# Graph attention, two layers: 52 instead of 46 edge tiles of layer 1 gathered early, their completion seven groups apart instead of eight

## The chip, the cores and the metric

The kernel runs on one core of one Trainium2 chip. The metric is the device time of one execution in microseconds (us). Nine runs of the kernel before gave a median of 2495.17 us, from 2488.37 to 2499.84. Engines are named as the profile names them: PE (TensorE matmul), PEld (TensorE weight load), DVE (VectorE), ACT (ScalarE), POOL (GpSimd), SP (SyncE, which here only issues DMAs).

## The reference, cut to what matters

6250 nodes with 768 features, 100,000 edges sorted by destination. Two layers of graph attention (4 heads, then 1), then a small MLP and a residual. A layer is:

```python
h = (x @ W).reshape(n, heads, -1)
e = leaky_relu(alpha_s[src] + alpha_d[dst], 0.2)
e = exp(e - segment_max(e, dst)[dst])
alpha = e / segment_sum(e, dst)[dst]
out = segment_sum(h[src] * alpha[:, :, None], dst)
```

The costly part is `h[src]`: for each of 100,000 edges a row of the layer's node table has to be fetched (268 numbers in layer 1, 259 in layer 2), weighted and added into its destination.

## The kernel before, in words

Nodes are cut into NT = 49 tiles of 128, edges into 782 tiles of 128. Four edge tiles make a **group** (196 groups per layer), two edge tiles a **pair**, and four groups belong to about one node tile, as edges are sorted by destination.

**Feature stage** (0 to about 172 us in the profile). For each node tile PE multiplies the normalised features with W1 (L457), ACT leaves the row in SBUF (`kept`, one tile for each node tile), and SP stores it to the layer's table in HBM (L484).

**Layer 1** (about 176 to 1309 us). POOL gathers the rows of each edge tile with one indirect DMA (L663), eight groups (AHEAD) before they are used, into a ring of 20 pair buffers `G`. DVE computes each pair's weights (L741, L751) and the weighted rows `hw` (L753, a ring of 8 pairs), and one-hot matrices of the destinations (`hot`, L691). PE adds each edge tile into its destinations with a one-hot matmul into `o_ps` (L765); an fp32 matmul is two MATMUL and two LDWEIGHTS records in the trace. Once in four groups PE also sums the destinations' factors with 16 small matmuls (`meet`, L709), and the node steps turn a finished node tile into its row for layer 2 (L963, L1016 and further). A buffer of G is free when DVE has made `hw` from it; a buffer of `hw` is free when PE has read it.

**Early gathers, the part that is changed.** While the features are still being computed, POOL has nothing else to gather. Some pairs of layer 1, listed in SOON, are therefore gathered then (`soon_rows`, L351, L357) from the part of the table that is already there: the entry SOON[i] = NT - m says that the last m node tiles are missing. Indices into the missing tiles are replaced by 0 (`soon_places`, L345). What is gathered is held in G buffers (16 pairs, SOON_HELD) or moved to HBM by SP (`soon_away`, L361, L364), all of it by the start of layer 1, and brought back by SP when its pair is due (`soon_back`, L366), so POOL skips that pair in `gather` (L651). What is missing is then added from `kept`, once for each of the pair's two edge tiles:

- `soon_hits` (L377, L383, DVE): m one-hot matrices of 128x128 that say which edge wants which node of a missing tile
- `soon_missing` (L388, L394, PE): m fp32 matmuls of 128x128 by 128x268 over the missing node tiles
- `soon_out` (L397, L400, ACT) copies the sum out of PSUM, and `soon_whole` (L402, L406, DVE) adds it to the gathered row.

The order on every engine is written out by hand in the loop over groups. SOON_GROUP[i] is the group whose second pair is the early pair i and at which its rows are made whole. Around it (`at`), the loop has:

```python
for k, hits_at in ((2 * i, at - 10), (2 * i + 1, at - 6)):
    if g == hits_at + 3 + (k % 2 == 0): soon_out(sm, k)
    if g == at: soon_whole(G, k)
    if g == hits_at: soon_hits(pre_pool, k)
    if g == hits_at + 1 + (k % 2 == 0): soon_missing(k)
if g == at - 13: soon_sources(pre_pool, i)
```

PSUM for `missing1`, for the node steps' `tp` and for their `h_ps` is one set of two buffers (tag "n").

**Layer 2** (about 1309 to 2475 us) gathers its 782 tiles in the same way (eleven of them early, in another manner, L334), puts the weight into the one-hot (L748), and ends each node tile with the MLP (L1129, L1139) and the output.

Of the kernel before, what the change touches and what calls it, by code (L numbers as in the profile page):

```python
# [27 lines left out]
NT = -(-N // P)  # L28
# [20 lines left out]
THERE = {layer: [there for n, there in stages for _ in range(n)] for layer, stages in EARLY.items()}  # L49


SOON = [NT - m for m in (11, 20, 2, 19, 11, 18, 3, 18, 4, 17, 4, 16, 5, 15, 10, 15, 7, 14, 13, 12, 9, 8,
                         6)]
SOON_GROUP = [8 * i + 11 for i in range(len(SOON))]
SOON_AT = {2 * g + 1: i for i, g in enumerate(SOON_GROUP)}
SOON_FROM, SOON_HELD = min(SOON), 16
BARE = 8
# [14 lines left out]
def kernel(  # L72
# [142 lines left out]
    def edge_places(ones):  # L215
# [5 lines left out]
        yield  # L221
        soonest = sorted(range(len(SOON)), key=SOON.__getitem__)
        for i in range(0, len(SOON), 2):
            for k in soonest[i:i + 2]:
# [112 lines left out]

    soon_i = const.tile([P, len(SOON), 2], I32, name="soon_i")
    soon_ok = const.tile([P, len(SOON), 2], F32, name="soon_ok")
    soon_d = dram.tile([len(SOON), P, 2 * TW[1]], F32, name="soon_d")  # L340
# [293 lines left out]
    def layer_edges(layer, H, node, pre, matched, pre_pool):  # L634
# [4 lines left out]
        with tc.tile_pool(name=f"eg{layer}", bufs=6) as eg, \  # L639
# [237 lines left out]
            for g in range(NG):  # L877
# [41 lines left out]
                if layer == 1:  # L919
                    for i, at in enumerate(SOON_GROUP):  # L920
                        for k, hits_at in ((2 * i, at - 10), (2 * i + 1, at - 6)):
# [565 lines left out]
```

## Time and profile before

| what | us |
|---|---|
| median of 9 runs | 2495.17 |
| the profiled execution's own time | 2497.29 |
| its span, first to last instruction | 2495.5 |
| around the span | 1.8 |
| PE busy, whole span | 1752.0 (70%) |
| POOL busy, whole span | 1526.4 (61%) |
| DVE busy, whole span | 1391.2 (56%) |
| ACT busy, whole span | 445.3 (18%) |

A row of the costliest groups gives line, engine and operation, tiles, shape and count, then the time the group was busy, the mean of one in ns, and after a second bar the engine's idle time just before these instructions with what ended it. "issue" there means that nothing which the profile shows was waited for, and "remote" that the releaser is not known. The mean granted TensorE clock of the whole run is 0.798 of full speed. Busy time of POOL is the gather instruction alone (0.95 us); between two gathers that wait for nothing lie another 0.30 us.

### The profile page before, as it was taken

The page shows a single profiled execution, that of the slowest core. Times are in us where ns is not written, and L with a number is a line of the kernel's source. Part 1 is how long each engine was busy: PE and PEld are TensorE (multiplying, and loading weights), DVE is VectorE, ACT ScalarE, POOL GpSimd, SP SyncE. Part 2 cuts the span into 40 slices and gives each one's busy share as a digit, 9 for nine tenths or more (in the row PEclk, how much of TensorE's full clock was granted, in tenths as well). Part 3 has the DMA queues.
Part 4 walks back from the last instruction along what each step waited for, and adds up shares of the span by engine and source line. Part 5 has one row for each costly group of instructions (what it writes and reads, how often), then busy time and mean ns, then how long its engine had stood idle before and what let it go on. Part 6 is the DMA issues. An engine that isn't in the chain of part 4 may idle for free.

```text
span 2495.5 us, 27029 instructions
## 1 busy us (share of the span) xinstructions
PE 1752.0 (70%) x7728; PEld 1280.3 (51%) x7729; DVE 1391.2 (56%) x4195; ACT 445.3 (18%) x1368; POOL 1526.4 (61%) x1666
## 2 busy tenths in 40 slices
PE   9961777777677775766674666676777677677677
PEld 7741555565465564655552444454454444444455
DVE  7742667666776676776772534443443444444444
ACT  6740011111111111111120011111111111111112
POOL 5257566666666666666625666666666666666661
PEclk9975888788788787887886767877876777777788
DMA  9986454555555554555524445544554545554552
GB/s 343 352 273 221 133 156 138 156 155 145 151 162 163 158 157 135 160 162 154 152 72 147 130 135 153 159 142 144 159 153 133 159 136 150 154 150 140 148 152 74
DMA packets 167330, 400.38 MB, mean 160 GB/s; under 512 B 36631, under 2 KB 54254, under 8 KB 167174
## 3 DMA queue, kind: packets, MB, share of 16 engines
q0 software_dynamic: 75072, 211.10, 31.9%
q1 hardware_dynamic: 90732, 185.99, 21.6%
q10 hardware_dynamic: 1370, 1.48, 0.2%
q8 instruction: 65, 1.06, 0.2%
q14 instruction: 91, 0.75, 0.1%
HBM read 333.87 MB, written 64.56 MB: 160 GB/s over the span
## 4 chain that ended last, share of the span: by engine, by line
PE 52%; issue 21%; DVE 11%; another core or an unknown queue 11%; ACT 3%; DMA 1%; POOL 1%; DVEq 0%; ACTq 0%; SPq 0%; POOLq 0%
PE o_ps L765 27%; PE missing L394 9%; PE y_ps L1139 6%; PE h_ps L457 4%; DVE hw L753 2%; PE tp L1129 2%; DVE hot L691 2%; DVE hw L748 1%; PE h_ps L1016 1%; PE e_parts L709 1%; PE y_ps L1078 1%; DVE factors L741 1%; DVE factors L751 1%; DVE acc L782 1%
## 5 line engine op out<-in xcount | busy, mean ns | idle before, releaser
L663 POOL DMA_INDIRECT G<-table,src_i x1507 | 1434.7, 952 | 788.6 <-issue 379.6
L765 PE MATMUL o_ps<-G,hw 128*128 128x258 f32 x1564 | 526.4, 463 | 223.7 <-issue 191.0
L765 PEld LDWEIGHTS o_ps<-G,hw 128*128 128x128 f32 x1564 | 350.4, 231 | 366.6 <-issue 275.6
L765 PE MATMUL o_ps<-hw,hot 128*128 128x260 f32 x1564 | 441.4, 423 | 104.6 <-issue 91.0
L753 DVE TENSOR_TENSOR hw<-G,factors 128x520 f32<-128x520 f32 x391 | 272.2, 696 | 287.5 <-remote 194.9
L765 PEld LDWEIGHTS o_ps<-hw,hot 128*128 128x128 f32 x1564 | 319.4, 209 | 187.9 <-issue 114.8
L394 PE MATMUL missing<-kept,soon_hit 128*128 128x268 f32 x1028 | 273.6, 416 | 64.0 <-issue 46.0
L748 DVE TENSOR_SCALAR hw<-iota_ps,dcol,w 128x128 f32<-128x128 f32 x782 | 284.9, 406 | 15.6 <-DVE w L744 1.3
L394 PEld LDWEIGHTS missing<-kept,soon_hit 128*128 128x128 f32 x1028 | 207.3, 204 | 118.0 <-issue 73.8
L791 ACT ACTIVATE sum<-acc 32x260 f32<-32x260 f32 (+1 forms) x384 | 160.0, 417 | 408.3 <-DVE acc L782 212.4
L1143 DVE TENSOR_TENSOR y<-y_ps,xt 128x384 f32<-128x384 f32 (+1 forms) x98 | 54.5, 556 | 265.5 <-PE o_ps L765 89.6
L1139 PE MATMUL y_ps<-wm,mT 128*128 128x384 f32 x392 | 184.1, 600 | 20.0 <-ACT mT L1134 12.2
L709 PE MATMUL e_parts<-win,mask 128*128 128x12 bf16 (+1 forms) x1564 | 68.2, 167 | 173.4 <-issue 169.3
L709 PEld LDWEIGHTS <-mask 128*128 128x128 bf16 x1564 | 61.8, 98 | 186.0 <-issue 174.6
L457 PE MATMUL h_ps<-w,r 128*128 128x264 f32 (+1 forms) x588 | 142.9, 398 | 14.8 <-issue 8.3
L691 DVE TENSOR_TENSOR hot<-iota_ps,dcol 128x512 f32<-128x512 f32 x196 | 133.5, 681 | 0.0
L457 PEld LDWEIGHTS h_ps<-w,r 128*128 128x128 f32 x588 | 111.9, 197 | 38.6 <-issue 10.0
L1139 PEld LDWEIGHTS y_ps<-wm,mT 128*128 128x128 f32 x392 | 78.3, 222 | 99.0 <-issue 54.1
L741 DVE TENSOR_TENSOR factors<-G,factors 128x8 f32<-128x8 f32 (+1 forms) x782 | 125.4, 160 | 4.4
L1134 ACT ACTIVATE mT<-tp,bm1c 128x128 f32<-128x128 f32 x98 | 30.6, 363 | 521.6 <-PE o_ps L765 175.5
L969 ACT ACTIVATE rT<-tp,bT 128x128 f32<-128x128 f32 x196 | 61.1, 364 | 277.9 <-remote 214.1
L782 DVE SCALAR_TENSOR_TENSOR acc<-acc,keep,o_ps 128x260 f32<-128x260 f32 (+1 forms) x192 | 91.3, 476 | 12.3 <-PE o_ps L765 7.7
(418 smaller groups left out, 1290.4 us busy)
## 6 DMA issues: line engine op xcount, KB each, us to landing
xt<-in_x SPq DMA_DIRECT2D x96, 384.0 KB
drow<-dmod_d SPq DMA_DIRECT2D x49, 512.0 KB
mask_d<-mask SPq DMA_DIRECT2D x97, 256.0 KB
mask<-mask_d SPq DMA_DIRECT2D x97, 256.0 KB
G<-table,src_i POOLq DMA_INDIRECT x1507
xTt<-in_xT SPq DMA_DIRECT2D x49, 384.0 KB
out<-y SPq DMA_DIRECT2D x48, 384.0 KB
table<-kept SPq DMA_DIRECT2D x49, 134.0 KB
```

The costliest lines, as they stand in the source:

```text
L394: nc.tensor.matmul(soon_p[k], hit[:, T - there], kept[T], start=(T == there), stop=(T == NT - 1))
L457: nc.tensor.matmul(h_ps[:, :n], r[:, k], w1[:, k, :n], start=(k == 0), stop=(k == KI - 1))
L663: nc.gpsimd.indirect_dma_start(out=G[k // 2][:, k % 2], out_offset=None, in_=table[layer], in_offset=bass.IndirectOffsetOnAxis(ap=src_i[:, ...
L691: nc.vector.tensor_tensor(hot[g][:, T[0]:T[0] + n], iota_ps.unsqueeze(1).to_broadcast([P, n, P]), dcol[:, k:k + n].unsqueeze(2).to_broadca ...
L709: nc.tensor.matmul(parts[t][:, at + k], m[:, k * P:(k + 1) * P], pre.win[:, 2 * u + 2], start=True, stop=True)
L741: nc.vector.tensor_mul(v, e2, rho)
L748: nc.vector.tensor_scalar(hw[:, t], iota_ps, dcol[:, k:k + 1], w[:, t], ALU.is_equal, ALU.mult)
L753: nc.vector.tensor_mul(hw, Gp[:, :, :RW[1]].rearrange("p t (h c) -> p t h c", h=H), w.unsqueeze(3).to_broadcast([P, 2, H, C + 1]))
L765: nc.tensor.matmul(o_ps[u], l, r[:, :RW[layer]], start=(g % 2 == 0 and k == 0), stop=(g % 2 == 1 and k == tiles(g)[-1]))
L782: nc.vector.scalar_tensor_tensor(acc, run[0], keep[:, u % 2:u % 2 + 1], o_ps.pop(u), ALU.mult, ALU.add)
L791: nc.scalar.activation(done[t][r], acc[r], AF.Copy)
L1139: nc.tensor.matmul(y_ps, mT[:, j], wm2[:, j, s * half:(s + 1) * half], start=False, stop=(j == KH - 1))
```

## The change

Three entries are added to SOON and the list is arranged anew; the early pairs stand 7 instead of 8 groups apart. Nothing else in the code is changed.

```diff
-SOON = [NT - m for m in (11, 20, 2, 19, 11, 18, 3, 18, 4, 17, 4, 16, 5, 15, 10, 15, 7, 14, 13, 12, 9, 8,
-                         6)]
-SOON_GROUP = [8 * i + 11 for i in range(len(SOON))]
+SOON = [NT - m for m in (11, 20, 2, 20, 3, 19, 4, 18, 4, 18, 5, 17, 7, 17, 10, 16, 11, 15, 15, 14, 13, 13,
+                         12, 9, 8, 6)]
+SOON_GROUP = [7 * i + 11 for i in range(len(SOON))]
```

That makes 26 pairs (52 edge tiles) instead of 23 (46). The missing node tiles add up to 307 instead of 257, so `soon_missing` has 614 matmuls instead of 514. The most for one pair stays 20, so the buffers keep their sizes. The early pairs stand in groups 11 to 186 (11 to 187 before). On POOL the compiled program has 52 early gathers (46) and 730 gathers in layer 1 (736); the gathers of layer 2 are unchanged. On SP it has three more stores of early rows, three more loads of them and three more loads of source indices.

## The prediction

> **What bounds the kernel now.** I read the busy table by stretches first, then the gather row and the matmul rows of the costliest groups, then the waits of PE and of DVE, then PE and POOL side by side in order of time. The first view is busy time by stretches: three of layer 1 (early, middle, late), then three of layer 2; the number behind an engine's time counts its instructions.
>
> ```profile
> core 0: us, PE busy (x) PEld busy (x) DVE busy (x) ACT busy (x) POOL busy (x), PEclk, DMA share, GB/s
> 260.00:600.00 340.00, 254.74 (x1155) 197.06 (x1154) 232.81 (x593) 48.29 (x161) 215.15 (x226) 0.82 0.53 149
> 600.00:930.00 330.00, 243.75 (x1149) 191.10 (x1148) 226.46 (x592) 52.74 (x182) 209.74 (x221) 0.83 0.55 157
> 930.00:1272.00 342.00, 232.84 (x1134) 189.04 (x1133) 232.73 (x611) 51.65 (x178) 219.02 (x231) 0.82 0.53 150
> 1371.00:1700.00 329.00, 224.05 (x919) 147.84 (x919) 148.01 (x560) 43.63 (x114) 216.95 (x228) 0.76 0.49 144
> 1700.00:2050.00 350.00, 250.62 (x1028) 167.27 (x1028) 157.10 (x596) 51.32 (x135) 229.95 (x242) 0.76 0.50 148
> 2050.00:2440.00 390.00, 274.49 (x1165) 183.78 (x1164) 174.73 (x658) 59.84 (x159) 255.49 (x270) 0.78 0.51 151
> ```
>
> No engine is full in any stretch. Now the waits, PE's and then DVE's, from 260 to 1260 us (us in total, times, longest).
>
> ```profile
> PE e_parts L709 <- issue: 120.4, 84, 2.6
> PE o_ps L765 <- issue: 72.9, 58, 2.4
> PE missing L394 <- issue: 46.0, 47, 2.2
> ...
> PE o_ps L765 <- DVE hw L753: 1.7, 1, 1.7
> ```
> ```profile
> DVE hw L753 <- remote: 183.1, 41, 7.1
> DVE hw L753 <- PE o_ps L765: 37.6, 15, 5.8
> ```
>
> PE hardly waits for DVE's `hw`; DVE waits for PE to free `hw` buffers; POOL's extra waits are for G buffers, on DVE. So everything hangs on PE, and PE's idle time is "issue": nothing that it waits for. What that is shows in order of time, PE then POOL:
>
> ```profile
> 1021.91 1.92 PE L765 MATMUL o_ps<-hw,hot 128*128 128x260 f32 x8
> 1023.67 0.27 PE L709 MATMUL e_parts<-win,mask 128*128 128x12 bf16 x5
> 1025.62 0.17 PE L709 MATMUL e_parts<-win,mask 128*128 128x12 bf16 x1 [1.68 <-issue]
> ...
> 1036.15 0.17 PE L709 MATMUL e_parts<-win,mask 128*128 128x12 bf16 x1 [1.24 <-issue]
> 1038.24 0.27 PE L709 MATMUL e_parts<-win,mask 128*128 128x12 bf16 x4 [1.92 <-issue]
> ```
> ```profile
> 1034.18 0.94 POOL L663 DMA_INDIRECT G<-table,src_i  x1 [0.30 <-issue]
> 1039.41 0.94 POOL L663 DMA_INDIRECT G<-table,src_i  x1 [4.28 <-DVE hw L753]
> ```
>
> From 1023.9 PE crawls, 0.7 to 2.8 us from one small matmul to the next, and at 1038.2 it is back at full pace, 3.1 us after POOL fell idle at 1035.1 because its ring was full. The same order returns at almost every long crawl (stalls that end at 680.4, 948.4, 993.7, 1127.9; POOL idle from 676.9, 945.4, 990.5, 1124.8). After a POOL pause PE runs about 100 to 140 records, then crawls until the next pause. So POOL's time and the pauses that PE needs make the length. That gives a law to calculate with: a gather costs 1.25 us (0.95 busy and 0.30 between), and the rest of a stretch is pause. By the six rows: 340 - 226 x 1.25 = 57.5 us for 2309 PE and PEld records, 24.9 ns a record; then 53.8 for 2297 (23.4), 53.3 for 2267 (23.5), 44.0 for 1838 (23.9), 47.5 for 2056 (23.1), 52.5 for 2329 (22.5). Two layers with different PE work agree within a tenth: 308.6 us for 13,096 records, **23.6 ns of pause for each PE record**.
>
> **The change part by part.**
>
> *Removed: six gathers of layer 1* (736 to 730) on POOL's path: 6 x 1.25 = **-7.5 us**.
>
> *Added: 100 matmuls of missing tiles* (514 to 614), each two MATMUL and two LDWEIGHTS records, 400 in all: 400 x 23.6 ns = **+9.4 us**. No row shows this price by itself, so both ends: below, 0, as the seven cycles between long crawls from 934 to 1245 us last 42.2 to 46.7 us and do not follow the number of missing tiles in them. Above, all of it on PE: the row of L394 has 273.6 us for 1028 MATMUL records, 266 ns each, 200 x 266 = 53 us. I take the law, since its six rows are nearest.
>
> The Trainium skill, "Runtime: NRT & Kernel Launch", section "Instruction fetch mechanics", says that an engine's instructions are streamed in 16 KiB blocks of 256 by a queue of its own while earlier ones run, so that crossing a block is mostly hidden. The trace agrees on the blocks (queue q8 has 65 packets, 1.06 MB), but not that PE's issue is smooth. By that rule the 400 records would cost nothing and the sum below would be -4.1 us instead of +5.3.
>
> *Moved into the feature stage: six early gathers and three stores to HBM.* 6 x 134 KB and 3 x 268 KB are 1.6 MB. From 100 to 150 us the DMA share is 0.99 to 1.01 at 304 to 341 GB/s, so at most 1.6 MB / 341 GB/s = 4.7 us; at least 0, for POOL has some 20 us of waits beyond the 0.30 between its early gathers (100.5 to 172.3 us), and the share is 0.72 from 150 on. From 100 to 172 us PE is busy 57.5 of 72 us, and one tile's twelve matmuls at 135 us take 5.65 instead of 2.84 us: 17 us lost, while the 46 gathers and seven stores move 8.0 MB; the same share for 1.6 MB is 17 x 1.6 / 8.0 = **+3.4 us**, which I take. Each added row waits for its table store, as before; what queues behind the stores on SP are the later x loads and table stores, and they are inside this price.
>
> *Beside other work:* DVE's `soon_hits`, 75.2 us for 514 matrices, 146 ns each, 100 more are 14.6 us; six L406 at 486 ns, 2.9 us. DVE has 183 + 38 us of waits for PE in this stretch; without that cover they would cost the 17.5 us. ACT: six copies of 393 ns, ACT is busy 165.5 us of layer 1's 1115.7. SP's three loads back and three of indices, 1.2 MB at a DMA share of 0.53. A load back waits for a G buffer, and SP's mask stores and `drow` loads queue behind it, but POOL waits for the same ring, and `drow` comes four node tiles ahead.
>
> *The new distance.* With 8 groups the early pairs stand at one phase to the node steps (every 4 groups), with 7 it drifts. Both use PSUM tag "n", where PE's waits for ACT in layer 1 are 10.6 + 5.4 + 5.0 = 21 us. They could vanish or double, so +-21; I take 0, as PE time that is not in the pause law is taken back from the crawl.
>
> Sum: -7.5 + 9.4 + 3.4 = **+5.3 us**. The profiled execution took 2497.3, so 2502.6 in its frame; it stood 2.1 above the median, so **2501 us** against 2495.17. About 0.2% (5 us) is what a measurement can tell from no change.
>
> **The rivals.**
>
> *A, faster: the pauses belong to POOL's full ring, not to PE's records.* The ring fills whether or not PE has more to do, the added matmuls only shorten the crawl that would come anyway, and the six gathers are pure gain. For it: the cycles above do not shrink when the missing tiles fall from 27 to 14 a cycle; the crawls grow instead (14.0 to 16.8 us). Against it: the same 23.6 ns in layer 2, where no tile is missing. It decides where a record costs under (7.5 - 3.4) / 400 = 10 ns. Price: -7.5 and nothing in the feature stage, 2488; if each of the three pairs also spares a wait of its own of 2.5 us, 2480.
>
> *B, slower: the pauses belong to the early pairs.* From 1024 on each 8-group cycle has one pause of about 4.3 us at the crawl and one of about 3 us after the skipped pair, some 7 us together beyond the 0.30s. With 26 cycles instead of 23: 3 x 7 = +21, -7.5, +3.4 = +17, 2512.
>
> *C, much slower: PE is the plain bound.* For it: PE has work at all times. Against it: the cycles do not follow the missing tiles. +53, nothing from POOL, +3.4: 2551.
>
> *The change does not do what it says:* the compiled program has the 52, 730 and 614, so no more than its effect is open.
>
> **How the numbers follow.** Forecast 0.46 (own range 2493 to 2512), A 0.27, B 0.18, C 0.08, something else 0.01. Slower by over 0.2%: 0.30 of the forecast's 0.46, and B and C, 0.56. Faster: 0.22 of A's 0.27 and 0.03 of the forecast's, 0.25. Within: the rest, 0.19. The range takes in the forecast, A to near its far end, and B with room for waits on PSUM (2512 + 16), and leaves out C: 2482 to 2528.
>
> **What would show it.** In the profile after, POOL's layer-1 row has 730 gathers at 952 ns; its pauses in layer 1 should be near 23.6 ns times PE's records, some 9 us more than now. The feature stage should end (first gather of layer 1, now at 176.1 us) 0 to 5 us later. If the pauses do not grow, A holds; if they grow by 15 us or more, with about three more pauses of 3 us after skipped pairs, B; if POOL's idle time grows by some 50 us while crawls stay as long, C. Wrong would be the forecast as a whole if layer 2, which nothing touches, changed by more than 5 us, or if the ends of the feature stage moved by 10.

## The result, and the profile after

| | before | after |
|---|---|---|
| median, us (runs) | 2496.08 (62) | 2526.94 (19) |
| lowest to highest, us | 2487.46 to 2516.34 | 2515.75 to 2539.88 |
| ratio after to before, 95% interval | | **1.0124 [1.0111, 1.0136]** |
| profiled execution, us | 2497.29 | 2520.74 |
| its span, us | 2495.5 | 2519.0 |
| mean granted TensorE clock | 0.798 | 0.805 |

The change costs 1.24%, 31.0 us of 2496 (27.7 to 33.9). The forecast was 2501, its range 2482 to 2528. (The profiled execution after stands 6.2 us below its median.) Where the 23.5 us between the two spans lie, counted from POOL's gathers in the two traces (us):

| stretch | before | after | difference |
|---|---|---|---|
| start to first gather of layer 1 | 176.1 | 191.3 | +15.2 |
| first to last gather of layer 1 | 1095.1 | 1109.4 | +14.3 |
| last of layer 1 to first of layer 2 | 49.7 | 48.9 | -0.8 |
| first to last gather of layer 2 | 1122.0 | 1121.6 | -0.4 |
| last gather to the end | 52.6 | 47.8 | -4.8 |

In this pair of traces the loss is in the two stages that the change touches, half and half, and layer 2 stands still. One pair doesn't settle the halves: in a second trace of the changed kernel, on another chip (after_same_chip, 2536.48 us), the first gather of layer 1 comes at 182.1, +6.0, and layer 1 takes 1131.2, +36.1; layer 2, at 1122.8, stands still there too. First layer 1, busy time by stretches, the same three as before (columns as above):

```profile
260.00:600.00 340.00, 256.74 (x1168) 198.69 (x1168) 230.08 (x583) 46.42 (x154) 207.91 (x218) 0.82 0.51 147
600.00:930.00 330.00, 255.57 (x1167) 198.01 (x1168) 229.43 (x577) 50.74 (x173) 206.41 (x217) 0.84 0.52 151
930.00:1272.00 342.00, 272.18 (x1239) 208.87 (x1238) 236.72 (x605) 53.10 (x182) 212.32 (x222) 0.83 0.53 152
```

In the same 1012 us POOL issues 657 gathers instead of 678, and PE executes 7148 records instead of 6873. What the gathers leave free is 340 - 218 x 1.25 = 67.5 us for 2336 records, 58.8 for 2335 and 64.5 for 2477, together 190.8 us, **26.7 ns a record**; before it was 164.6 us for 6873, 23.9. PE's waits and then DVE's, 260 to 1260 us:

```profile
PE missing L394 <- issue: 123.8, 111, 2.2
PE o_ps L765 <- issue: 48.1, 45, 3.3
PE e_parts L709 <- issue: 30.1, 29, 2.0
```
```profile
DVE hw L753 <- remote: 127.6, 35, 8.4
DVE hw L753 <- PE o_ps L765: 93.5, 27, 12.8
```

The sum of the three "issue" rows has fallen from 239 to 202 us, but it has changed its place: it fell on the small `e_parts` matmuls (120.4), and now it falls on the matmuls of missing tiles (123.8 instead of 46.0). DVE waits for PE as long as before (221; the "remote" waits of L753 are for a semaphore that PE alone raises). In the page's costliest groups the same row stands out:

```profile
L663 POOL DMA_INDIRECT G<-table,src_i x1501 | 1432.0, 954 | 810.2 <-issue 383.0
...
L394 PE MATMUL missing<-kept,soon_hit 128*128 128x268 f32 x1228 | 373.4, 449 | 131.9 <-issue 128.2
```

The gathers are six fewer at 954 ns. L394 has 200 records more and 99.8 us more busy time, 373.4 instead of 273.6. At the 266 ns of before, 200 records would be 53 us; the rest is the crawl, which now runs through these rows, with the half clock that comes with it. In order of time, PE and then POOL:

```profile
1027.14 1.60 PE L394 MATMUL missing<-kept,soon_hit 128*128 128x268 f32 x5
1029.78 0.47 PE L394 MATMUL missing<-kept,soon_hit 128*128 128x268 f32 x1 [1.04 <-issue]
1031.87 0.60 PE L394 MATMUL missing<-kept,soon_hit 128*128 128x268 f32 x1 [1.62 <-issue]
...
1038.88 0.60 PE L394 MATMUL missing<-kept,soon_hit 128*128 128x268 f32 x1 [1.49 <-issue]
1040.28 6.39 PE L394 MATMUL missing<-kept,soon_hit 128*128 128x268 f32 x18 [0.80 <-issue]
```
```profile
1041.27 0.94 POOL L663 DMA_INDIRECT G<-table,src_i  x1 [3.74 <-DVE hw L753]
```

POOL's idle time began at 1041.27 - 3.74 = 1037.5; at 1040.3, 2.8 us later, PE is back at full pace. It is the sequence that the prediction showed at 1024 to 1038, on other matmuls.

Now the feature stage, busy time by stretches of 20 us, before and then after:

```profile
100.00:120.00 20.00, 17.47 (x78) 13.73 (x77) 13.48 (x28) 13.64 (x43) 12.55 (x13) 1.00 1.02 353
120.00:140.00 20.00, 13.39 (x50) 10.76 (x51) 10.60 (x25) 9.19 (x32) 12.29 (x13) 0.86 0.99 293
```
```profile
100.00:120.00 20.00, 14.13 (x64) 11.35 (x63) 11.03 (x21) 11.23 (x36) 14.15 (x14) 0.91 1.02 340
120.00:140.00 20.00, 9.25 (x24) 7.02 (x24) 5.04 (x14) 4.95 (x15) 9.98 (x11) 0.59 0.58 178
```

From 120 to 140 us PE has 24 matmul records instead of 50, and the DMA engines, which the prediction took for the limit, are at 0.58 and 178 GB/s (0.58 and 177 in the second trace). What PE, POOL, ACT and DVE do there, and PE and POOL at 169 us (after):

```profile
119.66 4.62 PE L457 MATMUL h_ps<-w,r 128*128 128x264 f32 x12 [5.80 <-ACT r L447]
124.11 0.27 PE L439 MATMUL mean_ps<-ident,mv 128*128 128x128 f32 x1
135.13 5.40 PE L457 MATMUL h_ps<-w,r 128*128 128x264 f32 x12 [10.75 <-ACT r L447]
...
169.64 2.84 PE L457 MATMUL h_ps<-w,r 128*128 128x264 f32 x12
```
```profile
128.96 0.95 POOL L357 DMA_INDIRECT G<-table,soon_i  x1 [0.30 <-issue]
137.00 0.94 POOL L357 DMA_INDIRECT G<-table,soon_i  x1 [7.09 <-DVE bp L192]
...
169.52 0.94 POOL L357 DMA_INDIRECT G<-table,soon_i  x1 [0.30 <-issue]
```
```profile
132.96 0.47 ACT L462 ACTIVATE kept<-h_ps,rstd 128x256 f32<-128x256 f32 x1 [13.35 <-remote]
133.05 0.95 DVE L445 TENSOR_TENSOR cent<-xTt,mean_ps 128x768 f32<-128x768 f32 x1 [12.82 <-remote]
```

Two things are slow here. A node tile's twelve matmuls take 5.40 us instead of 2.84, and that is the granted clock, 0.50 from 135 to 140 us; in the prediction's row of 5.65 us it was 0.50 as well (135 to 141 us of before). The early gathers don't slow them: from 163 to 173 us POOL issues gathers without a pause, the clock is at 1.00, and a tile's twelve take 2.84 us. The larger part is lost between two tiles. PE's records end at 124.4, but ACT (L462) and DVE (L445), which wait for a semaphore that PE raises, start only at 132.96 and 133.05, 3.0 us after POOL's last gather ended at 129.9; then the next tile's matmuls can begin, at 135.13. What holds PE up from 124.4 on the trace doesn't show. Here it ends some 3 us after POOL fell idle, as the crawl of layer 1 does, with early gathers in the part of the gathers. That it is the same thing is argued, not shown: in the second trace PE's records of a tile end at 117.3, ACT starts only at 123.7, and POOL issues gathers without a pause all the while, to 127.4.

### The profile page after: what moved, and what is told of

It is laid out like the page before. It is cut to its first block, busy times and chain, and to the rows that moved or that the text cites. A ratio compares the mean times of both kernels' runs of the same rounds, so it can differ in the third digit from the quotient of the medians.

```text
span 2519.0 us, 27515 instructions
## 1 busy us (share of the span) xinstructions
PE 1804.8 (72%) x7928; PEld 1319.4 (52%) x7929; DVE 1408.7 (56%) x4213; ACT 447.5 (18%) x1374; POOL 1530.2 (61%) x1666
## 4 chain that ended last, share of the span: by engine, by line
PE 53%; issue 22%; DVE 11%; another core or an unknown queue 8%; DMA 2%; ACT 2%; POOL 1%; DVEq 0%; SPq 0%; ACTq 0%; POOLq 0%
PE o_ps L765 25%; PE missing L394 12%; PE y_ps L1139 5%; PE h_ps L457 4%; DVE hw L748 2%; DVE hw L753 2%; PE tp L1129 1%; PE y_ps L1078 1%; POOL G L663 1%; PE h_ps L1016 1%; DVE hot L691 1%; DMA G<-table,src_i 1%; DVE factors L741 1%; PE e_parts L709 1%
## 5 line engine op out<-in xcount | busy, mean ns | idle before, releaser
L765 PE MATMUL o_ps<-G,hw 128*128 128x258 f32 x1564 | 514.4, 458 | 218.4 <-issue 161.6
L765 PE MATMUL o_ps<-hw,hot 128*128 128x260 f32 x1564 | 418.8, 408 | 80.3 <-issue 63.3
L394 PE MATMUL missing<-kept,soon_hit 128*128 128x268 f32 x1228 | 373.4, 449 | 131.9 <-issue 128.2
L753 DVE TENSOR_TENSOR hw<-G,factors 128x520 f32<-128x520 f32 x391 | 272.2, 696 | 306.4 <-remote 141.9
L765 PEld LDWEIGHTS o_ps<-hw,hot 128*128 128x128 f32 x1564 | 306.8, 201 | 156.6 <-issue 94.4
L394 PEld LDWEIGHTS missing<-kept,soon_hit 128*128 128x128 f32 x1228 | 266.7, 220 | 231.3 <-issue 177.8
L1139 PE MATMUL y_ps<-wm,mT 128*128 128x384 f32 x392 | 177.1, 580 | 27.2 <-issue 14.4
L457 PE MATMUL h_ps<-w,r 128*128 128x264 f32 (+1 forms) x588 | 144.6, 402 | 24.6 <-ACT r L447 19.7
L457 PEld LDWEIGHTS h_ps<-w,r 128*128 128x128 f32 x588 | 112.9, 199 | 48.4 <-ACT r L447 21.6
L709 PE MATMUL e_parts<-win,mask 128*128 128x12 bf16 (+1 forms) x1564 | 62.7, 167 | 100.5 <-issue 93.1
L1129 PE MATMUL tp<-rT,wm 128*128 128x128 f32 x392 | 64.2, 314 | 55.9 <-ACT rT L969 33.4
```

The source lines that it names most:

```text
L394: nc.tensor.matmul(soon_p[k], hit[:, T - there], kept[T], start=(T == there), stop=(T == NT - 1))
L457: nc.tensor.matmul(h_ps[:, :n], r[:, k], w1[:, k, :n], start=(k == 0), stop=(k == KI - 1))
L709: nc.tensor.matmul(parts[t][:, at + k], m[:, k * P:(k + 1) * P], pre.win[:, 2 * u + 2], start=True, stop=True)
L753: nc.vector.tensor_mul(hw, Gp[:, :, :RW[1]].rearrange("p t (h c) -> p t h c", h=H), w.unsqueeze(3).to_broadcast([P, 2, H, C + 1]))
L765: nc.tensor.matmul(o_ps[u], l, r[:, :RW[layer]], start=(g % 2 == 0 and k == 0), stop=(g % 2 == 1 and k == tiles(g)[-1]))
L1129: nc.tensor.matmul(m_ps[:, j], wm1[:, k, j * P:(j + 1) * P], rT[:, k], start=(k == 0), stop=(k == KH - 1))
```

## The experiments

Ratios are against runs of the kernel before on the same chip, with 95% intervals; on the chip of the first four it took 2522.62 us, on the others 2496.6 to 2499.92. An amount in us is the ratio's excess times that time.

After the result I had three explanations. **The sum**: the forecast's law (a gather 1.25 us, PE's records a pause each) with terms of the wrong size. **The distance**: seven groups apart is what costs. **POOL is innocent**: its gathers lie in time that it has to spare, and PE alone sets layer 1, so nothing was gained for the loss. The last is what the first four experiments suggested, and the second round was made for it.

### Each part alone: e1, e2, e3, e4

e1, before's 46 tiles at the new distance:
```diff
-SOON_GROUP = [8 * i + 11 for i in range(len(SOON))]
+SOON_GROUP = [7 * i + 11 for i in range(len(SOON))]
```


> The list of before (46 tiles, 514 matmuls of missing tiles), only set seven groups apart, so that the last pair stands in group 165. Budget theory (PE runs some 110 to 140 records after each pause of POOL and then crawls until the next one; a record costs 24 ns of pause): the same gathers and records, so no change, 2496 us within 6. Pair theory (each early pair brings pauses of some 7 us): the same 23 pairs, so no change either. Distance theory (the loss in layer 1 comes from the seven groups, which drift against the node steps): 2508 to 2515 us.

e2, before with 100 more matmuls of the same shape, whose sums the following start=True throws away:
```diff
+            for _ in range(3 if k < 8 else 2):
+                nc.tensor.matmul(soon_p[k], hit[:, 0], kept[there], start=True, stop=True)
             for T in range(there, NT):
```


> Before, with the first matmul of the missing tiles issued two or three times more for each edge tile, 100 more in all (400 PE records) that are overwritten; gathers, stores and DVE as before. Budget theory: 400 x 24 ns = 9 us more, 2505 us, all of it between the first and the last gather of layer 1. Pair theory: no pair more, 2496 us. PE as the plain bound: 200 MATMUL records at 226 to 266 ns, 45 to 53 us more, 2541 to 2549 us.

e3, before with three more pairs gathered early (and moved to HBM like the others), which nothing reads (the diff is cut; `soon_d` also gets room for three more):
```diff
+        again = {NT - 20: 1, NT - 17: 9, NT - 13: 18}
+        if there in again:
+            i, extra = again[there], len(SOON) + sorted(again).index(there)
+            soon_G[extra] = rows_in(1)
+            for t in range(2):
+                nc.gpsimd.indirect_dma_start(out=soon_G[extra][:, t], ...)
```


> Before, with three more pairs gathered in the feature stage (where 20, 17 and 13 node tiles are missing, as the change adds them) and stored by SP, and never used: layer 1 keeps its 736 gathers and 23 pairs. Budget theory (a run of early gathers without a pause of POOL makes PE crawl in the feature stage too): the first gather of layer 1 comes 8 to 15 us later than at 176, 2504 to 2511 us. Bytes theory (only the DMA time of 1.6 MB): 3 to 5 us later, 2499 to 2501 us. Hidden: no change.

e4, after with 514 matmuls; the first two or three missing node tiles of most edge tiles are left out of the sum:
```diff
-            for T in range(there, NT):
+            left = 3 if NT - there == 20 else 2 if NT - there > 3 else 0
+            for T in range(there + left, NT):
```


> After, with 100 matmuls left out (the first two missing node tiles of each edge tile, three where twenty are missing, none where two or three are), so that 514 are left as before; the rows of these tiles are left out of the sum. Gathers, stores and DVE as after. Budget theory: 9 us less than after, 2517 us. Pair theory: as after, 2527 us. PE as the plain bound: 45 to 53 us less than after, 2474 to 2482 us.

| kernel | median, us | ratio | us against before |
|---|---|---|---|
| e1, distance alone | 2536.59 | 1.0040 [1.0018, 1.0062] | +10.1 (4.5 to 15.6) |
| e2, matmuls alone | 2537.10 | 1.0058 [1.0039, 1.0076] | +14.6 (9.8 to 19.2) |
| e3, early gathers alone | 2533.13 | 1.0032 [1.0014, 1.0050] | +8.1 (3.5 to 12.6) |
| e4, after without 100 matmuls | 2541.36 | 1.0067 [1.0046, 1.0088] | +16.9 (11.6 to 22.2) |

Each part costs. The three add up to 32.8 us, which is what the whole change takes (31.0), so there seemed to be nothing left that the six saved gathers bring; and after without the matmuls is 0.57% below after, 14 us, the same as e2 above before. Rival C (53 us for the matmuls) falls.

### Does POOL's time count: p1, p2, p3 and after_same_chip

POOL gets a memset of its own of 128x512 after every eighth gather (194 of them; p1 on before, p2 on after), or two of them (p3, on before). after_same_chip is after unchanged, for p2. The diff is cut to what follows each gather:
```diff
+        gathers.append(1)
+        if len(gathers) % 8 == 0:
+            for _ in range(1):          # p3: range(2)
+                nc.gpsimd.memset(hush, 0.0)
```


> Before, with one 128x512 memset on POOL after every eighth gather (early ones, layer 1 and layer 2; 194 in all); nothing else. A 128x128 memset takes 0.20 us in the profile of before, so some 0.7 us each, 140 us on POOL. Budget theory (PE runs 110 to 140 records after a pause of the gathers and then crawls until the next pause): with a pause every 10 us, in which PE needs some 80 records, the crawls go, and with them the 171 us that POOL stands at its full ring in layer 1 and some 160 us in layer 2, as far as PE's own work allows: 330 - 140 = 190 us less at best, so 2310 to 2450 us. Rival (the crawls end with POOL's pause only because both hang on the same ring): the memsets are hidden in POOL's idle time or add up to 140 us: 2496 to 2640 us.

> After, with the same memset after every eighth gather. Budget theory: as much faster as before gets by it, and the difference between the two kernels shrinks from 31 us to what six gathers save and 400 PE records cost without crawls (-8 to +10 us), since the feature stage no longer has 28 us of early gathers without a pause. Rival: after stays 31 us behind before.

> Before, with two such memsets after every eighth gather, some 1.4 us. Budget theory: if one memset is too short to count as a pause, this one is long enough (PE's crawls have ended by pauses of 1.1 us and more): 2350 to 2480 us; if one was enough, 130 us slower than with one. Rival: slower than before by up to 280 us.

> The changed kernel once more, on the chip of these runs, so that traces and ratios stand beside each other: 1.0124 times before by every theory.

| kernel | median, us | ratio |
|---|---|---|
| p1, before with one memset | 2489.84 | 0.9964 [0.9949, 0.9978] |
| p3, before with two | 2494.24 | 0.9990 [0.9967, 1.0013] |
| p2, after with one memset | 2523.07 | 1.0093 [1.0064, 1.0123] |
| after_same_chip | 2530.45 | 1.0116 [1.0081, 1.0151] |

The memset row of the page and POOL's waits from 260 to 1260 us, both of p3:

```profile
L346 POOL MEMSET hush<- 128x512 f32 x388 | 208.5, 537 | 11.2
```
```profile
POOL G L674 <- issue: 163.0, 546, 1.1
POOL G L674 <- DVE factors L753: 39.5, 34, 4.2
POOL G L674 <- DVE hw L765: 37.2, 27, 3.7
```

208.5 us more work on POOL and no loss. Its waits for free G buffers fall from 97.7 + 63.2 us in before (hw, factors) to 37.2 + 39.5. Counted over layer 1, what POOL idles beyond the 0.30 us goes from 171 us to 133 (p1) and 76 (p3); with the 50 and 104 us of layer 1's memsets added it is 183 and 180. So a memset goes into the pauses and leaves their sum nearly as it was. That pauses put in by hand would make crawls go away altogether, the strict form of the forecast's law (2310 to 2480 us were expected), fell; p1, at 0.9964, has the lowest ratio of this study, p2 can't be told from after.

I took this for proof that POOL is innocent. It is not: a memset is not a gather.

### The test that settled it: x2

Every eighth edge tile of layer 1 is gathered a second time into a tile that nothing reads, 98 gathers:
```diff
+                    if layer == 1 and k % 8 == 1:
+                        nc.gpsimd.indirect_dma_start(
+                            out=again, out_offset=None, in_=table[layer],
+                            in_offset=bass.IndirectOffsetOnAxis(ap=src_i[:, k:k + 1], axis=0))
```


> The kernel before, every eighth edge tile of layer 1 gathered a second time into a buffer that nothing reads: 98 more gathers, 13 MB more from the table. If a gather costs 1.25 us on POOL's path (the forecast's first term): +122 us, ratio 1.049, and POOL's extra idle time in layer 1 stays at 171 us. If POOL's gathers only fill pauses: within 0.4% of before, and the extra idle time falls from 171 us to some 50. If it is the bytes that count: the DMA share in layer 1 rises from 0.53 to 0.6, PE's loads of data do not wait for it, so little.

2629.22 us, **1.0529 [1.0496, 1.0562]**: +132 us (124 to 140) for 98 gathers, **1.35 us each** (1.26 to 1.43). Busy time by stretches, and the page's row of the added gathers, x2:

```profile
260.00:600.00 340.00, 225.94 (x1019) 174.36 (x1018) 200.72 (x508) 41.44 (x138) 215.97 (x227) 0.79 0.51 144
600.00:930.00 330.00, 216.22 (x974) 170.38 (x974) 203.66 (x533) 45.39 (x157) 211.84 (x223) 0.79 0.52 148
930.00:1272.00 342.00, 238.53 (x1081) 186.01 (x1081) 210.62 (x543) 47.98 (x166) 219.84 (x232) 0.80 0.52 149
```
```profile
L668 POOL DMA_INDIRECT again<-table,src_i x98 | 93.1, 950 | 29.9 <-issue 29.9
```

227, 223 and 232 gathers where before had 226, 221 and 231: the gathers of a stretch stay the same, though an eighth of them is useless, and it is PE that gets less done (2037 records instead of 2309 in the first stretch). DMA share and GB/s don't rise, so it is not the bytes. Layer 1 from first to last gather is 134.4 us longer, 98 x 1.25 = 122.5 of gathers and 11.6 of pauses (182.4 instead of 170.8). So time without gathers is what PE needs, it can be idle or a memset, and a gather takes 1.25 us away from it. "POOL is innocent" has fallen; the forecast's first term stands.

### Taking early pairs away: x1

```diff
-SOON = [NT - m for m in (11, 20, 2, 19, 11, 18, 3, 18, 4, 17, 4, 16, 5, 15, 10, 15, 7, 14, 13, 12, 9, 8, 6)]
+SOON = [NT - m for m in (11, 2, 11, 3, 4, 4, 5, 15, 10, 15, 7, 14, 13, 12, 9, 8, 6)]
```


> The kernel before without the six early pairs that lack 16 to 20 node tiles: 17 pairs, 8 groups apart as before. 12 more gathers in layer 1, 216 matmuls (864 records of PE) and 108 one-hot matrices fewer, 12 early gathers and 4 to 6 stores fewer in the feature stage. By the forecast's law: 12 x 1.25 = +15.0, 864 x 23.6 ns = -20.4, feature stage 2 x -3.4 = -6.8, sum -12, ratio 0.995. If POOL's gathers lie on the path and the matmuls cost nothing (rival A): +15 - 7 = +8, ratio 1.003. If layer 1 goes by PE and POOL's gathers only fill pauses (the 100 matmuls alone took 14.6 us, 36 ns a record, and the gathers brought nothing): 864 x 36 ns = -31, the gathers 0, the feature stage -8 to -16: ratio 0.981 to 0.984, and POOL's extra idle time in layer 1, 171 us, falls by the 15 us of the gathers and by what layer 1 gets shorter. Then it is the version that beats both kernels.

2494.38 us, 0.9983 [0.9967, 0.9999]: -4.2 us (-8.2 to -0.2). In the profile the first gather of layer 1 is 3.1 us earlier (173.0), and layer 1 takes 1099.8 us, 4.7 more: 15.0 for the 12 gathers, -10.8 of pauses for 810 fewer records in it. From the time: -4.2 - 15.0 + 3.1 = -16.1 us for 864 records, 19 ns each. That hangs on the 3.1 us of one trace: by e3's price (8.1 us for six early gathers) the twelve would have brought 16 us, and next to nothing would be left for the records. None of the three sums of the expectation came out, the law's -12 (0.995) either. Rival B falls whichever price holds: six pairs fewer would save 6 x 7 us of pauses, -42 + 15 - 7 = -34. The version without early pairs of many missing tiles is as good as the one with them, hardly better.

### Place and distance: x3, x4

x3, before with its pairs two groups later:
```diff
-SOON_GROUP = [8 * i + 11 for i in range(len(SOON))]
+SOON_GROUP = [8 * i + 13 for i in range(len(SOON))]
```


> The kernel before, the early pairs made whole two groups later (8 i + 13 instead of 8 i + 11): the same number, the same distance of eight groups, another place against the node steps, which come every four groups. Seven groups apart, with the same 46 tiles, ratio 1.0040 over before less what chips differ, some 10 us. If that comes from the places against the node steps, which seven goes through evenly, the three other places cost 13 us on average, and this one should differ from before: 1.002 to 1.016. If it comes from the early pairs standing closer (26 matmuls more for each stretch of 8 groups, none in the last 31 groups): 0, ratio 0.999 to 1.001. The forecast, which took the distance for nothing: 0 in both.

2513.98 us, 1.0070 [1.0049, 1.0091]: **+17.5 us** (12.2 to 22.7) for the same work at the same distance. The longest of PE's waits from 260 to 1260 us, x3:

```profile
PE missing L394 <- issue: 168.0, 161, 3.0
```

The row of `e_parts`, 120.4 us in before, is gone, and that of `missing` went from 46.0 to 168.0: the place decides which matmuls the crawl falls on. Waits for ACT on PSUM, the mechanism behind the prediction's bound of 21 us, are not there (21 us in before, no row of 1.3 us or more here). PE's steps of 0.6 us and more from one record to the next, counted over layer 1 from its 61st gather on, take 409 us instead of 358.

x4, after with its 26 pairs at the places of before, 23 of them at 8 i + 11 and three between:
```diff
-SOON_GROUP = [7 * i + 11 for i in range(len(SOON))]
+SOON_GROUP = sorted([8 * i + 11 for i in range(23)] + [55, 111, 167])
```


> The kernel after with its 26 pairs at the places of the kernel before: 23 of them eight groups apart at 8 i + 11, and three between, at groups 55, 111 and 167, four groups from their neighbours, so that every pair stands at the same place of the four groups of a node tile. If the places against the node steps are what the new distance costs (seven apart with the 46 tiles 1.0040, two groups later with the 46 tiles 1.0070): after's 1.0124 less 0.004 to 0.007, so 1.005 to 1.008. What is left then has to be the sum of 100 matmuls (9.4 by the law, 14.6 measured alone), the feature stage (8 measured alone) and six gathers (-7.5 by the forecast, -8.1 by 98 gathers issued twice, which took 132 us), 9.3 to 15 us or 1.004 to 1.006. If the distance costs by how close the pairs stand, or if the three pairs four groups apart wait for PSUM: 1.012 or more.

2543.41 us, 1.0187 [1.0160, 1.0215]: slower than after: not the 1.005 to 1.008 that the places alone would give, but the last case of the expectation, 1.012 or more. DVE's waits from 260 to 1260 us, x4:

```profile
DVE soon_hit L383 <- remote: 31.6, 5, 8.0
DVE soon_hit L383 <- PE missing L394: 21.5, 4, 6.2
```

Neither row is there in before. `soon_hit` has two buffers (L382), and pairs four groups apart want three or four. The eight-group stretches that hold the three added pairs (from groups 48, 104 and 160) take 55.4, 57.9 and 56.8 us by DVE's `hw` instructions, 42.6, 45.6 and 44.7 in before: 37 of the 46.7 us. The other 9.5 would be within the 9 to 15 us that were expected of the same places without the distance, but that is a subtraction, not a run: x4 puts a wait in the place of the distance and tells nothing sure about it.

## Why the prediction was right or wrong

| step | forecast, us | measured, us | by |
|---|---|---|---|
| six gathers fewer | -7.5 | -8.1 (-8.6 to -7.6) | x2, 6 x 1.35 |
| 100 matmuls more | +9.4 | +14.6 (9.8 to 19.2) | e2; after less e4, 14.2 |
| into the feature stage | +3.4 | +8.1 (3.5 to 12.6) | e3 |
| new distance | 0 | +10.1 (4.5 to 15.6) | e1 |
| sum | +5.3 | +24.7 (16 to 33) | |
| the whole change | | +31.0 (27.7 to 33.9) | |

(The interval of the sum takes the four errors as independent.) The time fell into the range and on the side that was given 0.56; the forecast itself, 2501, was 26 us too low, and of the 31 us it had 5. That the range holds is in part luck: its upper end, 2528, was made for rival B with waits on PSUM, neither is what the runs show, and the measured time lies 1 us inside it.

- **What bounds the kernel**: right in its main point. "POOL's time and the pauses that PE needs make the length" is what x2, p1 and p3 show together, with one correction: it is the gathers' time that counts, not POOL's. Memsets are free in it, up to two after every eighth gather; 98 gathers cost 1.35 us each.
- **Six gathers, -7.5**: right.
- **100 matmuls, +9.4 by the law of 23.6 ns a record**: the mechanism held, the size was low: 14.6 us for 400 records are 37 ns (25 to 48); x1, taking 864 away, gives 19 or less. The price isn't a constant: over the traces of the kernels without memsets, the pauses of layer 1 are 24.2 (before) to 29.0 ns (x4) for each record of PE in it. Six rows of one profile agreed within a tenth and hid that. The Trainium skill ("Runtime: NRT & Kernel Launch", section "Instruction fetch mechanics") isn't contradicted by that: it says that crossing a block of instructions is mostly hidden, and in the traces of before and after none of the 53 crawls of over 6 us ends within 3 us after such a block has landed on PE's queue (q8). From that page alone the records would have had no price, and they measured 14.6 us.
- **The feature stage, +3.4**: this step failed in its reason, and its size was low, 8.1 us by e3. It was priced by bytes, at DMA engines taken as full, from the row of twelve matmuls in 5.65 instead of 2.84 us; that row is the granted clock at 0.50. In both traces of after the DMA engines are at 0.58 where the time goes, and what PE has to signal comes 6.4 to 8.6 us late beside early gathers. That gathers without a pause hold PE up is read from the trace, and no run takes it away: short memsets between the early gathers (p2) left the first gather of layer 1 at 189.4 us, where after has 182.1 on the same chip. Nor does e3 alone exclude the bytes, as its interval reaches down to 3.5. The stage's end scatters, one execution of each kernel: in five kernels whose feature stage is that of before the first gather of layer 1 comes at 168.8 (x3) to 184.9 us (e1), in five with 52 early gathers at 182.1 to 192.5 (e4). Before had pauses of 1.0 to 1.5 us between its early gathers, at 103.8, 115.1 and 118.8 us; e1, with the same 46, has none from 106.9 to 128.4. The prediction's condition for being wrong as a whole, an end of that stage moved by 10 us, was met in the first trace (the last L457 matmul at 181.9 instead of 171.2, the first gather 15.2 us later, not 0 to 5) and not in the second (173.4, and 6.0 later).
- **The new distance, 0 between -21 and +21**: this step failed. The cost of 10.1 us lies inside the bound, but the reason given for it (waits on PSUM) isn't what it is, as x3 shows; that "PE time that is not in the pause law is taken back from the crawl" is wrong, for the place decides where the crawl falls and how long it takes.
- **Pauses, some 9 us more**: 170.8 to 190.4 us in layer 1, +19.6, for 402 more records (7053 to 7455). At 23.6 ns these are 9.5 us; the other 10.1 is the higher price of each record, and of the same size as e1's cost of the distance. In the second trace the pauses are 213.8 us, 43 more, so what the forecast had at 9 is larger in both, by an amount that one trace doesn't give.
- **Rivals**: A fell by e2, where the matmuls alone cost 14.6 us, and so did C. B's sign was there (pauses 15 us or more longer, 72 pauses of over 1.1 us instead of 60, 66 in the second trace), but not its mechanism. e4, with 26 pairs and 514 matmuls, took 16.9 us (11.6 to 22.2), which agrees with B's 17 and, within the errors, with distance, feature stage and gathers without any price per pair (10.1 + 8.1 - 8.1 = 10.1, 3 to 17); it is x1 that tells them apart, with -4.2 where B has -34.
- **Open**: why PE's issue slows to a record every 0.7 us and more while gathers are issued one behind the other, and why one place of the early pairs makes more of it than another. What the traces do show: of the 53 crawls of over 6 us (steps of 0.6 us and more from one PE record to the next) from 250 to 1290 us of before and after, 51 end 0.7 to 4.6 us after a pause of POOL of over 1.1 us began, and none as a block of PE's instructions lands.

## What to carry to other kernels

When two engines look half idle, change one kind of work at a time on the suspect: 194 memsets said that POOL's time is free, 98 useless gathers said that gathers are not, and only both together name the resource. A price worked out as "rest of the stretch by count" is a mean under one arrangement of the work; before it is multiplied with a change, ask whether the change moves where the rest falls, and give that move a term of its own with a cost, not a zero with two signs. And price a stage that the change fills up by the waits that are seen there, not by the engine whose share reads 1.0; before a slow row of PE is put down to anything else, read the granted clock beside it.

## What the hardware showed that was not expected

- A node tile's twelve matmuls take 2.84 us at a granted clock of 1.00 and 5.65 at 0.50; gathers issued back to back beside them change nothing in that (after, 164 to 172 us). What came late beside such gathers is PE's semaphore: 8.6 us after PE's last record in after (124.4 to 133.0 us), 6.4 in its second trace (117.3 to 123.7).
- A POOL memset of 0.54 us after every eighth gather makes the kernel 0.36% faster (0.22 to 0.51); two of them (1.13 us together) make no difference that was measured.
- The granted clock follows the crawl. In before PE crawls from 664.6 to 680.4 us, and the clock is at 0.5 from 670.3 to 684.0, 5.7 and 3.6 us behind; from the 61st gather of layer 1 on, steps of 0.6 us and more take 358 us and the half clock 358; in x3 they are 409 and 395, in after 334 and 345. The clock falls after the crawl has begun and comes back after it has ended, so the half clock is not what starts it.
- One chip took 2522.62 us for the kernel before where others took 2496.6 to 2499.92; that 1% is more than most parts of this change, so only ratios on one chip were compared.
